# A graph kernel's ending: the flag of odd entries a block earlier, the last rows in two parts

## Chip, cores and metric

The kernel runs on one core of a Trainium2 chip. The metric is the device time of one execution in microseconds (us), the median of several runs. A profile is one execution recorded by the hardware profiler; its times within the execution are counted from the span's start. The engines are TensorE (PE, its weight loads PEld), VectorE (DVE), ScalarE (ACT), GpSimd (POOL) and SyncE (SP).

## The reference

Four graph layers act on x (4096 rows of 64) through one 4096 x 4096 adjacency matrix. Each layer normalizes x, puts the result through ReLU to get h, and adds a term to x. The first three are an attention over the neighbours, a sum over the last 100 neighbours with weights that halve, and a product of h with adj @ h. The last one matters here:

```python
deg = jnp.sum(adj, axis=1, keepdims=True)
nb_agg = adj @ X / jnp.maximum(deg, 1.0)
X_cat = jnp.concatenate([X, nb_agg], axis=1)
out = X_cat @ W.T
return jax.nn.relu(out)
```

Here X is h of layer 3 (layers are numbered from 0) and the result is added to x. The entries of the drawn adjacency are 0 and 1, but the function is defined for any numbers.

## The kernel before

The kernel computes the layers on the assumption that all entries of adj are 0 or 1, and checks this as it goes. Whole-matrix checks on VectorE (`check`, L351) count in a tile `odd` the entries that are neither. At the end `flagged` (L1081 to L1090) sums `odd` over its columns on VectorE (L1084, tile `bad`), over the partitions with a matmul on PE (L1088, tile `pf`), and cuts that down to 0 or 1 on VectorE (L1090, tile `flag`). Each engine then loads `flag` into a register (`values_load`, L1448) and branches (`tc.If`, L1449): if it is 1, the whole model is computed again by a general version, `model(True)`, whose instructions stand between the branch and the end of the program. With the drawn inputs it is 0 and each engine jumps over them. L1495 is where the program ends: every engine drains, and they meet in a barrier.

The 4096 destination rows are worked in 8 blocks of 512 (NIB = 8), numbered 0 to 7 as in the code; so the sixth block is `ib` 5. Layer 3 adds, for each block, 32 products into one PSUM bank (`acc`, L1293), each of 128 x 128 weights with 512 columns of the mask. Blocks 0 to 3 are begun together with a skew of four products; blocks 4 to 7 follow one after the other. When a block's sum is complete, `done3` (L1427) pushes a job, `rows3`, that turns it into 512 rows of output:

- ACT copies and scales `acc` from PSUM to SBUF (`evacuated`, L213)
- PE transposes it in four parts (`turned`, L229)
- ACT copies that to SBUF (L235) and GpSimd adds its two halves (L237): the products are made with numbers split in two parts
- VectorE multiplies by the reciprocal degrees (L1397), GpSimd adds the rows' own term (L1400), VectorE applies ReLU and adds x (L1402)
- GpSimd issues the store (L1403)

For block 7 (`final`) PE does the transposing and the adding of the halves in one, with a constant matrix `fold` (L227), VectorE multiplies straight from PSUM, and SyncE issues the store.

The jobs are Python generators, and the order of instructions on every engine is the order in which these generators emit them. `product` calls `beat` after every fourth product, and `beat` calls `step` (L302). A step advances the jobs in the queue from the front by one `yield` each; a job pushed with a lag of 4 lets no later job run in its first three steps. After the last product, `drain` steps until no job is left. An engine works through its instructions in that order; one that waits holds up all that are queued behind it on the same engine.

`done3` pushes the flag job when block 6 (`NIB - 2`) is complete, after emptying the list of checks. The job yields 12 times between L1084 and L1088. The register is loaded after `model(False)` has returned, behind everything else.

Of the kernel before, what the change touches and what calls it, by code (L numbers as in the profile page):

```python
# [11 lines left out]
F32 = mybir.dt.float32  # L12
# [4 lines left out]
AF = mybir.ActivationFunctionType  # L17
ALU = mybir.AluOpType
# [5 lines left out]
D = 64  # L24
P = 128
NT = N // P
IB = 512
NIB = N // IB
CI = IB // P
# [19 lines left out]
def kernel(  # L49
# [12 lines left out]
    nc = tc.nc  # L62
# [30 lines left out]
    fold = cpool.tile([P, D], F32, name="fold")  # L93
# [8 lines left out]
    part = cpool.tile([P, QUAD], BF16, name="part")  # L102
# [24 lines left out]
    def bc(col, r):  # L127

        return col.unsqueeze(2).to_broadcast([P, r, D])
# [4 lines left out]
    def model(general):  # L134

        sfx = "_g" if general else ""
        stack = ExitStack()

        def pool(name, bufs, on=stack, **kw):
            return on.enter_context(tc.tile_pool(name=name + sfx, bufs=bufs, **kw))  # L140
# [6 lines left out]
        x_sb = main.tile([P, NT, D], F32, name="x_sb" + sfx)  # L147
        fa = main.tile([P, NT, D], F32, name="fa" + sfx)
        rdegs = main.tile([P, NT], F32, name="rdegs" + sfx)
# [35 lines left out]
        epi = pool("epi", 1)  # L185
# [11 lines left out]
        def rows_tile(name, tag, on=epi, bufs=1, dtype=F32):  # L197
            return on.tile([P, CI, D], dtype, tag=name, name=f"{name}{tag}{sfx}", bufs=bufs)

        def small(name, tag, on=epi, n=CI):  # L200
            return on.tile([P, n], F32, tag=name, name=f"{name}{tag}{sfx}")

        def evacuated(ib, acc, layer, scale=None, vector=False, third=False):
            on, bufs = (evac, 1) if third else (epi, 2)
            asb = on.tile([P, IB], F32, tag="asb", name=f"asb{layer}_{ib}{sfx}", bufs=bufs)
            if scale is None:
                nc.scalar.copy(asb, acc)
            elif vector:
                nc.vector.tensor_scalar(asb, acc, scale, None, ALU.mult)
            elif isinstance(scale, float):  # L210
                nc.scalar.activation(asb, acc, AF.Copy, scale=scale)
            else:
                nc.scalar.activation(asb, acc, AF.Identity, scale=scale)  # L213
            return asb

        def turned(asb, b, tag, adding=False):


            shape = (P, CI, D if adding else P)
            if b is None:  # L220
                pt = pm.tile(list(shape), F32, tag="pr", name=f"pt{tag}{sfx}")
            else:
                pt = bank(b, f"pt{tag}", shape)
            for c in range(CI):
                part = asb[:, c * P : (c + 1) * P]
                if adding:
                    nc.tensor.matmul(pt[:, c, :], part, fold, start=True, stop=True)  # L227
                else:
                    nc.tensor.transpose(pt[:, c, :], part, ident)  # L229
            return pt  # L230

        def halves_added(to, asb, pt):

            v = asb.rearrange("p (c i) -> p c i", c=CI)
            nc.scalar.copy(v, pt)  # L235
            yield
            nc.gpsimd.tensor_tensor(to, v[:, :, 0:D], v[:, :, D:P], ALU.add)  # L237
            yield
# [59 lines left out]
        def push(job, lag):  # L298

            jobs.append([job, lag])  # L300
# [20 lines left out]
        def drain():  # L321
            while jobs:
                step()

        def block(ib):
            return slice(ib * CI, (ib + 1) * CI)
# [10 lines left out]
        def check(tiles=1):  # L337


            if not checks:  # L340
                return
            k = checks.popleft()
            ib, t = divmod(k, NT)
            if tiles == 2 and k % 2 == 0:
                checks.popleft()
                at = more[0].tile([P, CG, IB], F32, tag="ckw", name=f"ckw_{k}", bufs=more[1])
                nc.sync.dma_start(out=at, in_=adjt[ib, t // CG])
            else:
                at = ck.tile([P, IB], F32, tag="ck", name=f"ck_{k}", bufs=CHECKED)
                nc.sync.dma_start(out=at, in_=adjt[ib, t // CG][:, t % CG, :])  # L350
            nc.vector.scalar_tensor_tensor(  # L351
                at, at, 0.0, at, ALU.not_equal, ALU.not_equal, accum_out=odd[:, k : k + 1]
            )
# [655 lines left out]
        with tc.manual_schedule():  # L1009
            acc, late = first_rows_and_block()  # L1010
# [19 lines left out]
            for size in sizes:  # L1030
# [10 lines left out]
                for ib, g, att in late:  # L1041
                    at = done % NG
                    if at == 0:
                        acc = pa0.tile([P, IB], F32, tag="pa", name=f"acc0_{ib}{sfx}")
# [6 lines left out]
                late = now  # L1051
# [11 lines left out]
        evac = pool("evac", 1)  # L1063
# [4 lines left out]
        def bank(b, name, shape=(P, IB)):  # L1068
            return banks.tile(list(shape), F32, tag=f"bank{b}", name=name + sfx)
# [11 lines left out]
        def flagged(flag):  # L1081

            bad = small("bad", "")[:, 0:1]
            nc.vector.tensor_reduce(bad, odd, AX.X, ALU.add)  # L1084
            for _ in range(12):
                yield
            pf = pm.tile([P, CI], F32, tag="pr", name="pf")
            nc.tensor.matmul(pf[0:1, 0:1], bad, one, start=True, stop=True)  # L1088
            yield
            nc.vector.tensor_scalar(flag, pf[0:1, 0:1], 1.0, None, ALU.min)  # L1090
# [124 lines left out]
        with tc.manual_schedule():  # L1215
# [42 lines left out]
            late = None  # L1258
            for blocks in GROUPS:
                for k in range(NT // PAIR):  # L1260
                    t = NT - 1 - k * PAIR
# [5 lines left out]
                    late = units, ws  # L1267
# [8 lines left out]
        epi2 = pool("epi2", 1, l2)  # L1276
        stream2 = own_sb = v_sb3 = None
        if general:
            stream2 = pool("stream2", 2, l2)
            own_sb = epi2.tile([P, NT, D], F32, name="own" + sfx)  # L1280
# [28 lines left out]
        def sums(layer, s2, rows32, done, lead, split):  # L1309


            begun = {}
            for n in range(0 if general else split + SKEW * (lead - 1)):
                for ib in range(lead):
                    t = n - SKEW * ib
                    if t == 0:
                        begun[ib] = next_sum(layer, ib)
                    if 0 <= t < split:
                        product(begun[ib], ib, t, s2, layer)
            for ib in range(NIB):  # L1320
                if ib in begun:
                    acc = begun[ib]
                    products23(acc, ib, list(range(split, NT)), s2, rows32, layer)
                else:
                    acc = next_sum(layer, ib)
                    products23(acc, ib, list(range(NT)), s2, rows32, layer)
                done(ib, acc)
                if general:
                    drain()

        sums_level = 1.0 / UP if general else level[:, 1:2]
# [53 lines left out]
        def rows3(ib, acc):  # L1385
            tag = f"3_{ib}"
            rows = block(ib)
            asb = evacuated(ib, acc, 3, sums_level, third=ib % 3 == 2)
            yield
            yield  # L1390
            final = ib == NIB - 1
            pt = turned(asb, 3 + ib % 2, tag, final)
            yield
            y = rows_tile("y", tag, epi2, 2)
            if not final:
                yield from halves_added(y, asb, pt)
            nc.vector.tensor_tensor(y, pt if final else y, bc(rdegs[:, rows], CI), ALU.mult)  # L1397
            yield
            own = (own_sb if general else fa)[:, rows, :]
            nc.gpsimd.tensor_tensor(y, y, own, ALU.add)  # L1400
            yield
            nc.vector.scalar_tensor_tensor(y, y, 0.0, x_sb[:, rows, :], ALU.max, ALU.add)  # L1402
            (nc.sync if ib == NIB - 1 else nc.gpsimd).dma_start(out=out[:, rows, :], in_=y)  # L1403

        def degrees(ib):

# [12 lines left out]
            nc.vector.reciprocal(to, to)  # L1419
            nc.vector.tensor_scalar(to, to, turn_v, None, ALU.mult)  # L1420

        flag = None
        with tc.manual_schedule():
            def done2(ib, acc):
                push(rows2(ib, acc), 6)

            def done3(ib, acc):  # L1427
                nonlocal flag
                push(rows3(ib, acc), 4)
                if ib == NIB - 2 and not general:  # L1430
                    while checks:
                        check(2)
                    flag = cpool.tile([1, 1], I32, name="flag")
                    push(flagged(flag), 1)

            sums(2, s2b, fa, done2, 4, 24)
            if general:
                for ib in range(NIB):
                    degrees(ib)
            often[:] = [True, True, False]  # L1440
            sums(3, s2a, v_sb3, done3, 4, 28)
            drain()
        l2.close()
        stack.close()
        return flag

    flag = model(False)
    any_odd = nc.values_load(flag[0:1, 0:1], min_val=0, max_val=1)  # L1448
    with tc.If(any_odd > 0):  # L1449
        model(True)  # L1450


# [47 lines left out]
```

## Time and profile before

| what | value |
|---|---|
| median of 3 runs | 631.16 us (629.65 to 631.86) |
| the profiled execution | 627.16 us |
| its span | 625.3 us |
| PE busy | 567.6 us (91%) |
| VectorE busy | 482.1 us (77%) |
| ACT busy | 337.4 us (54%) |
| GpSimd busy | 228.2 us (36%) |
| HBM read | 135.63 MB |

The span runs from the first to the last instruction of the profile; the execution takes a little longer. Busy time leaves out waiting and the instructions that only steer: register loads, branches, semaphores, the issuing of DMAs. Two sides of an engine are told apart in the profile: `ACT` is the engine at work, `ACTq` its sequencer, which fetches and issues the instructions. A line such as `pt<-fold,asb 128*128 128x64 f32 x8` names the tile written, the tiles read, the shapes and how many instructions are merged. What stands in brackets behind a line of the timeline is the idle time of the engine before it and what ended that.

### The profile page before, as it was taken

What the parts mean: (1) busy time and instruction counts of PE and PEld (TensorE: products, weight loads), DVE (VectorE), ACT (ScalarE), POOL (GpSimd) and SP (SyncE); (2) the same over time, 40 slices, a digit from 0 to 9 for tenths busy, and PEclk for the clock granted to TensorE, in tenths of its full rate; (3) what the DMA queues carried; (4) which work ended last, traced back from release to release, by engine and by line L of the source; (5) the groups of instructions that cost most, each with busy time, mean ns of one, the idle gap of its engine ahead of it and who ended that gap; (6) DMA issues with size and microseconds to landing.
All of it is one profiled execution on the core that took longest, in us unless ns stands there. A gap on an engine that the chain in (4) does not pass through costs nothing.

```text
span 625.3 us, 9033 instructions
## 1 busy us (share of the span) xinstructions
PE 567.6 (91%) x2997; PEld 230.8 (37%) x3012; DVE 482.1 (77%) x945; ACT 337.4 (54%) x541; POOL 228.2 (36%) x462
## 2 busy tenths in 40 slices
PE   0767999999999999999998999999989999998993
PEld 0653223333333333323343343343434445443551
DVE  5768558998888888888968767868776769988741
ACT  1467567666666676766615667767765024331320
POOL 7423301665656564733336300101000325442352
PEclk9995999999999999999999999999999999999997
DMA  8992914698999898972276332323334575468911
GB/s 138 141 104 18 105 16 85 101 150 140 159 143 159 140 156 139 144 147 84 85 264 207 108 130 101 135 103 123 113 104 132 176 262 180 160 208 303 327 42 32
DMA packets 43640, 87.03 MB, mean 139 GB/s; under 512 B 5216, under 2 KB 21984, under 8 KB 43584
## 3 DMA queue, kind: packets, MB, share of 16 engines
q1 hardware_dynamic: 24672, 68.53, 32.3%
q0 software_dynamic: 18768, 17.70, 30.2%
q8 instruction: 25, 0.41, 0.3%
q10 hardware_dynamic: 144, 0.13, 0.2%
q14 instruction: 31, 0.25, 0.1%
HBM read 135.63 MB, written 1.05 MB: 219 GB/s over the span
## 4 chain that ended last, share of the span: by engine, by line
PE 69%; DVE 11%; DMA 5%; POOL 5%; ACT 4%; issue 4%; SPq 0%; DVEq 0%; POOLq 0%; ACTq 0%
PE acc L1293 16%; PE ps L908 14%; PE acc L935 13%; PE acc L1223 8%; PE cnt L1185 8%; DMA mask<-adjt_dram 3%; PE cnt L1195 3%; DVE att L927 3%; DVE ckw L351 2%; PE pt L229 2%; ACT ps L914 2%; DVE ck L351 1%; PE ps_h L615 1%; DMA x_sb<-x_dram 1%; PE pr L1099 1%
## 5 line engine op out<-in xcount | busy, mean ns | idle before, releaser
L914 ACT ACTIVATE ps<-ps,att_c,att_a 128x1024 f32<-128x1024 f32 x128 | 146.9, 1176 | 83.1 <-PE ps L908 83.0
L927 DVE TENSOR_TENSOR att<-ps,mask 128x1024 f32<-128x1024 f32 x128 | 155.2, 1221 | 39.4 <-ACT ps L914 36.9
L908 PE MATMUL ps<-qt,kt 64*128 64x512 f32 x512 | 134.4, 633 | 4.9 <-DVE att L927 3.9
L351 DVE SCALAR_TENSOR_TENSOR ckw<-ckw 128x1024 f32<-128x1024 f32 x93 | 119.5, 1299 | 7.5 <-DMA ckw<-adjt_dram 7.4
L935 PE MATMUL acc<-att,fb 128*64 128x512 f32 x512 | 122.5, 605 | 0.7 <-DVE att L927 0.7
L1211 ACT ACTIVATE w<-cnt 128x512 int16<-128x512 f32 x176 | 93.1, 597 | 46.0 <-PE cnt L1195 45.7
L1209 DVE TENSOR_SCALAR w<-cnt 128x512 int16<-128x512 f32 x80 | 53.7, 688 | 34.7 <-PE cnt L1195 34.0
L176 POOL DMA_DIRECT2D mask<-adjt_dram x128 | 70.2, 561 | 20.3 <-DMA mask<-adjt_dram 18.6
L908 PEld LDWEIGHTS ps<-qt,kt 64*128 64x128 f32 x512 | 44.3, 188 | 86.6 <-DVE att L927 40.9
L1185 PE MATMUL cnt<-mask,after 128*128 128x512 fp8e4 x256 | 66.5, 379 | 4.4 <-DVE w L1209 3.9
L1223 PE MATMUL acc<-w,s2a 128*128 128x512 bf16 x241 | 64.1, 382 | 1.9 <-issue 1.6
L935 PEld LDWEIGHTS acc<-att,fb 128*64 128x64 f32 x512 | 31.8, 136 | 81.1 <-issue 76.6
L272 POOL TENSOR_TENSOR xc<-x_sb,st 128x256 f32<-128x256 f32 x24 | 19.1, 794 | 108.4 <-DVE st L269 67.5
L1293 PE MATMUL acc<-mask,s2b 128*128 128x512 fp8e4 x256 | 57.7, 379 | 0.0
L1293 PE MATMUL acc<-mask,s2a 128*128 128x512 fp8e4 x256 | 57.6, 380 | 0.0
L351 DVE SCALAR_TENSOR_TENSOR ck<-ck 128x512 f32<-128x512 f32 x70 | 50.6, 724 | 0.0
L258 POOL TENSOR_TENSOR rs_a<-rs_y 128x4 f32<-128x4 f32 x48 | 17.3, 359 | 88.7 <-DVE rs_y L254 81.0
L1185 PEld LDWEIGHTS <-after 128*128 128x128 bf16 x256 | 24.8, 99 | 33.6 <-issue 6.2
L1293 PEld LDWEIGHTS <-s2b 128*128 128x128 f16 x256 | 25.0, 98 | 27.6 <-issue 0.8
L1293 PEld LDWEIGHTS <-s2a 128*128 128x128 f16 x256 | 24.7, 98 | 27.5
L213 ACT ACTIVATE asb<-acc,level 128x512 f32<-128x512 f32 x24 | 16.1, 692 | 32.1 <-PE acc L1293 32.1
L1223 PEld LDWEIGHTS <-s2a 128*128 128x128 f16 x256 | 19.8, 97 | 29.8 <-issue 14.8
(188 smaller groups left out, 529.8 us busy)
## 6 DMA issues: line engine op xcount, KB each, us to landing
ckw<-adjt_dram SPq DMA_DIRECT2D x93, 512.0 KB, 3.8
ck<-adjt_dram SPq DMA_DIRECT2D x70, 256.0 KB, 5.8
mask<-adjt_dram POOLq DMA_DIRECT2D x128, 128.0 KB, 9.0
x_sb<-x_dram SPq DMA_DIRECT2D x4, 256.0 KB, 8.0
out_dram<-y POOLq DMA_DIRECT2D x7, 128.0 KB, 2.2
w_sb<-wts_dram SPq DMA_DIRECT2D x2, 80.0 KB, 7.7
vec<-vecs_dram ACTq DMA_DIRECT2D x1, 130.5 KB, 6.1
out_dram<-y SPq DMA_DIRECT2D x1, 128.0 KB, 1.9
```

The costliest lines, as they stand in the source:

```text
L176: nc.gpsimd.dma_start(out=masks[ib][:, g * CG : (g + 1) * CG, :], in_=adjt[ib, g])
L272: nc.gpsimd.tensor_tensor(xc, xr, bc(st, CI), ALU.add)
L351: nc.vector.scalar_tensor_tensor(at, at, 0.0, at, ALU.not_equal, ALU.not_equal, accum_out=odd[:, k : k + 1])
L908: nc.tensor.matmul(ps[:, c, :], kt[half, g, :], qts[ib][half, :], start=True, stop=True)
L914: nc.scalar.activation(ps, ps, AF.Sigmoid, bias=att_c, scale=att_a)
L927: nc.vector.tensor_tensor(att, ps, mask, ALU.mult)
L935: nc.tensor.matmul(acc[c * D : (c + 1) * D, :], lhs[:, t, :], rhs[:, c, :], start=(at == 0), stop=(at == NG - 1), skip_group_check=True,)
L1185: nc.tensor.matmul(cnt, after, masks[ib][:, t, :], start=True, stop=True, skip_group_check=True)
L1209: nc.vector.tensor_scalar(w, cnt, 0.0, None, ALU.max)
L1211: nc.scalar.activation(w, cnt, AF.Relu)
L1223: nc.tensor.matmul(accs[ib], both(s2a, t), w, start=(t == NT - 1), stop=False, skip_group_check=True,)
L1293: nc.tensor.matmul(acc, both(s2, t), masks[ib][:, t, :], start=(t == 0), stop=(t == NT - 1), skip_group_check=True,)
```

## The change

- The flag job is pushed when block 5 (`NIB - 3`) is complete, and yields 5 times between L1084 and L1088 where it yielded 12 times.
- Block 6 (`late`) has three yields fewer; its own rows are added by VectorE in place of GpSimd, and its store is issued by SyncE in place of GpSimd.
- Block 7 has a function of its own, `last_rows3`. ACT copies the first 256 columns of `acc`, VectorE the other 256. Then each engine loads the flag into its register. For each half PE folds two parts into a PSUM bank of its own, VectorE multiplies by the degree and adds the own term in one instruction for each 64 columns, applies ReLU and adds x in one for the half, and ACT issues the half's store.
- `tc.If` uses the registers that were loaded there.

The general model gets the same new functions; it isn't executed with these inputs.

```diff
@@ flagged
-            for _ in range(12):
+            for _ in range(5):
                 yield
@@ rows3
+            late = ib == NIB - 2
             asb = evacuated(ib, acc, 3, sums_level, third=ib % 3 == 2)
             yield
-            yield
-            final = ib == NIB - 1
-            pt = turned(asb, 3 + ib % 2, tag, final)
+            if not late:
+                yield
+            pt = turned(asb, 3 + ib % 2, tag)
             yield
             y = rows_tile("y", tag, epi2, 2)
-            if not final:
-                yield from halves_added(y, asb, pt)
-            nc.vector.tensor_tensor(y, pt if final else y, bc(rdegs[:, rows], CI), ALU.mult)
-            yield
+            yield from halves_added(y, asb, pt)
+            nc.vector.tensor_tensor(y, y, bc(rdegs[:, rows], CI), ALU.mult)
+            if not late:
+                yield
             own = (own_sb if general else fa)[:, rows, :]
-            nc.gpsimd.tensor_tensor(y, y, own, ALU.add)
-            yield
+            (nc.vector if late else nc.gpsimd).tensor_tensor(y, y, own, ALU.add)
+            if not late:
+                yield
             nc.vector.scalar_tensor_tensor(y, y, 0.0, x_sb[:, rows, :], ALU.max, ALU.add)
-            (nc.sync if ib == NIB - 1 else nc.gpsimd).dma_start(out=out[:, rows, :], in_=y)
+            (nc.sync if late else nc.gpsimd).dma_start(out=out[:, rows, :], in_=y)
+
+        def last_rows3(ib, acc):
...
+            half = slice(0, H * P)
...
+                nc.scalar.activation(asbs[0][:, half], acc[:, half], AF.Identity, scale=sums_level)
+            nc.vector.tensor_scalar(
+                asbs[1][:, half], acc[:, H * P :], sums_level, None, ALU.mult
+            )
+            if not general:
+                any_odd.append(nc.values_load(flag[0:1, 0:1], min_val=0, max_val=1))
+            yield
+            y = rows_tile("y", f"3_{ib}", epi2, 2)
+            for u in range(2):
+                rows = slice(ib * CI + u * H, ib * CI + (u + 1) * H)
+                pt = bank(3 + u, f"pt3_{ib}_{u}", (P, H, D))
+                for c in range(H):
+                    nc.tensor.matmul(
+                        pt[:, c, :], asbs[u][:, c * P : (c + 1) * P], fold, start=True, stop=True
+                    )
+                for c in range(H):
+                    t = ib * CI + u * H + c
+                    nc.vector.scalar_tensor_tensor(
+                        y[:, u * H + c, :], pt[:, c, :], rdegs[:, t : t + 1], own[:, t, :],
+                        ALU.mult, ALU.add,
+                    )
+                part = y[:, u * H : (u + 1) * H, :]
+                nc.vector.scalar_tensor_tensor(part, part, 0.0, x_sb[:, rows, :], ALU.max, ALU.add)
+                nc.scalar.dma_start(out=out[:, rows, :], in_=part)
@@ done3
-                push(rows3(ib, acc), 4)
-                if ib == NIB - 2 and not general:
+                push(last_rows3(ib, acc) if ib == NIB - 1 else rows3(ib, acc), 4)
+                if ib == NIB - 3 and not general:
                     while checks:
                         check(2)
                     flag = cpool.tile([1, 1], I32, name="flag")
@@ the program's end
-    flag = model(False)
-    any_odd = nc.values_load(flag[0:1, 0:1], min_val=0, max_val=1)
-    with tc.If(any_odd > 0):
+    any_odd = model(False)
+    with tc.If(any_odd[0] > 0):
         model(True)
```

More of the change, by code (lines that the diff above doesn't have):

```diff
@@ L1397, in rows3 @@
-            nc.vector.tensor_tensor(y, pt if final else y, bc(rdegs[:, rows], CI), ALU.mult)
-            yield
-            own = (own_sb if general else fa)[:, rows, :]
-            nc.gpsimd.tensor_tensor(y, y, own, ALU.add)
-            yield
-            nc.vector.scalar_tensor_tensor(y, y, 0.0, x_sb[:, rows, :], ALU.max, ALU.add)
-            (nc.sync if ib == NIB - 1 else nc.gpsimd).dma_start(out=out[:, rows, :], in_=y)
+            yield from halves_added(y, asb, pt)
+            nc.vector.tensor_tensor(y, y, bc(rdegs[:, rows], CI), ALU.mult)
@@ new lines, in rows3 @@
+            if not late:
+                yield
+            own = (own_sb if general else fa)[:, rows, :]
+            (nc.vector if late else nc.gpsimd).tensor_tensor(y, y, own, ALU.add)
+            if not late:
+                yield
+            nc.vector.scalar_tensor_tensor(y, y, 0.0, x_sb[:, rows, :], ALU.max, ALU.add)
+            (nc.sync if late else nc.gpsimd).dma_start(out=out[:, rows, :], in_=y)
+        def last_rows3(ib, acc):
+            own = own_sb if general else fa
+            H = CI // 2
+            asbs = [
+                on.tile([P, IB], F32, tag="asb", name=f"asb3_{ib}_{u}{sfx}", bufs=bufs)
+                for u, (on, bufs) in enumerate(((epi, 2), (evac, 1)))
+            ]
+            half = slice(0, H * P)
+            if general:
+                nc.scalar.activation(asbs[0][:, half], acc[:, half], AF.Copy, scale=sums_level)
+            else:
+                nc.scalar.activation(asbs[0][:, half], acc[:, half], AF.Identity, scale=sums_level)
[4 more added lines that the diff above has]
+                any_odd.append(nc.values_load(flag[0:1, 0:1], min_val=0, max_val=1))
+            yield
+            y = rows_tile("y", f"3_{ib}", epi2, 2)
[15 more added lines that the diff above has]
+                nc.scalar.dma_start(out=out[:, rows, :], in_=part)
@@ L1420, in degrees @@
             nc.vector.tensor_scalar(to, to, turn_v, None, ALU.mult)
-        flag = None
+        flag, any_odd = None, []
         with tc.manual_schedule():
@@ L1444, in model @@
         stack.close()
-        return flag
-    flag = model(False)
-    any_odd = nc.values_load(flag[0:1, 0:1], min_val=0, max_val=1)
-    with tc.If(any_odd > 0):
+        return any_odd
+    any_odd = model(False)
+    with tc.If(any_odd[0] > 0):
         model(True)
```

## The prediction

> **What bounds the kernel now.** I read the page first (PE busy 91%, and 0.3 of the last of the 40 slices), then the chain of waits from 612 us on. Blocks are numbered from 0, so the seventh is block 6. The matrix products end at 613.21; what follows is a chain of single instructions:
>
> ```profile
> 613.30 0.70 ACT asb L213
> ...
> 614.04 1.12 PE pt L227 x8
> ...
> 615.18 0.43 DVE y L1397
> ...
> 615.70 0.72 POOL y L1400
> ...
> 616.44 0.42 DVE y L1402
> 616.87 0.06 DVE flag L1090
> ```
>
> The chain ends 8.4 us before the span does (625.34). What fills that time are sequencer instructions, seen in the answers by line for L1448 (loads), L1449 (branch) and L1495 (end); columns: shortest/median/longest ns, then first and last start in us:
>
> ```profile
> L1448 ACTq TENSOR_LOAD <-flag x1: 465/465/465, 617.0 to 617.0; - x1
> ...
> L1448 SPq TENSOR_LOAD <-flag x1: 543/543/543, 617.3 to 617.3; - x1
> ```
>
> ```profile
> L1449 ACTq COMPARE_BRANCH  x1: 50/50/50, 617.5 to 617.5; - x1
> L1449 PEldq COMPARE_BRANCH  x1: 4502/4502/4502, 617.6 to 617.6; - x1
> ...
> L1449 SPq COMPARE_BRANCH  x1: 45/45/45, 618.6 to 618.6; - x1
> L1449 ACTq EVENT_SEMAPHORE  x1: 17/17/17, 620.3 to 620.3; - x1
> ...
> L1449 POOLq INC_SWDGE_SEM  x1: 782/782/782, 621.2 to 621.2; - x1
> ```
>
> ```profile
> L1495 POOLq DRAIN  x3: 46/107/2433, 622.1 to 625.1; - x3
> L1495 SPq DRAIN  x3: 7/7/13, 623.3 to 624.8; - x3
> ```
>
> Every engine loads the flag (0.47 to 0.54 us), branches over the general model, and does nothing for 2.8 us (ACT) to 4.5 us (PE); then GpSimd needs until 624.5 (INC_SWDGE_SEM 0.78, DRAIN 2.43), SyncE until 623.4, and the closing barrier takes 0.85 us. GpSimd ends this tail.
>
> **What the skill says.** "Runtime: NRT & Kernel Launch", Instruction fetch mechanics: a taken branch to a target outside the window waits for a DMA fetch. The trace agrees: after the branches the instruction queues move 9 packets of 8 KB and 2 of 16 KB. "Advanced Engine Details and Errata", Control Flow Timing, gives about 108 ns for a compare-and-branch; the four short ones here take 45 to 72. "TensorE: Matmul & The Clock Gate", What's actually happening: the clock falls after an idle window of about 3.4 us. The trace agrees that shorter gaps are harmless (last fence). "Perfetto Trace Analysis", Optimizing Scalar/DVE Operations: splitting instructions can let work finish sooner, at a fixed cost each. Here ACT's copy from PSUM takes 585 ns for 512 columns and 372 for 256, so 159 are fixed.
>
> **Part 1, the flag made a block earlier: it adds a wait on PE.** A step runs every fourth product. Block 5's row job is pushed with lag 4, the flag job behind it, so the sum L1084 falls in step 4 of block 6, and its PE matmul L1088, five steps later, in step 1 of block 7. L1402 is in the eighth step of a row job: block 4's job began in step 2 of block 5, so its L1402 is emitted in step 1 of block 6, block 5's in step 8. On VectorE the sum then stands behind the former, and VectorE is late, because GpSimd carries the row jobs one after another, 3.33 us each:
>
> ```profile
> 607.06 0.43 DVE L1402 SCALAR_TENSOR_TENSOR y<-y,x_sb 128x256 f32<-128x256 f32 x1 [0.84 <-POOL y L1400]
> ...
> 607.78 0.56 POOL L1403 DMA_DIRECT2D out_dram<-y  x1 [0.76 <-DVE y L1402]
> ...
> 608.28 0.60 PE L229 MATMUL pt<-ident,asb 128*128 128x128 f32 x4
> ...
> 610.40 0.43 DVE L1402 SCALAR_TENSOR_TENSOR y<-y,x_sb 128x256 f32<-128x256 f32 x1 [0.83 <-POOL y L1400]
> 610.74 0.41 DVE L1084 TENSOR_REDUCE bad<-odd 128x1 f32<-128x256 f32 x1
> 611.12 0.56 POOL L1403 DMA_DIRECT2D out_dram<-y  x1 [0.76 <-DVE y L1402]
> 611.70 0.73 POOL L237 TENSOR_TENSOR y<-asb 128x256 f32<-128x256 f32 x1
> ```
>
> The row at 607.06 is block 4's (GpSimd's stores leave in block order; the last, at 614.45, is block 6's). These lines are from the timeline; brackets give idle time before and what ended it. The sum follows such a row by 0.34 us: 607.40 to 607.81. PE reaches step 1 of block 7 eight products before the transposes of block 6 at 608.28 (step 3): 608.28 - 8 x 0.216 = 606.55. So PE stands at L1088 from 606.55 until 607.86, with all of block 7 behind it; the two passes of L1088 cost about 0.1 more (0.19 in all before, pipelined). PE loses 1.4 us: the products end at 613.21 + 1.4 = 614.6. Low 1.1 (if the first products are already queued in the pipe), high 1.6. The flag's own operation comes after 610.40 + 0.34, at 610.74, and no load of it is reached before 612.4: it makes nobody wait. The checks add nothing: the last one is on VectorE ahead of block 2's final operation, before block 5 ends.
>
> **Part 2, block 6's rows in fewer steps.** Its transposes move one step earlier and its own rows are added by VectorE; SyncE stores. GpSimd still adds the halves, in order at 611.70 to 612.43. VectorE follows with three dependent operations of 0.42 + 0.035: 612.47 to 613.81; SyncE issues the store (0.35) until 614.2. This lies under block 7's products. It frees GpSimd at 612.43 instead of 616.41 (its own issue took 0.56), and puts SyncE's load behind that store; nothing else stands in SyncE's queue, whose last loads for the checks are done by 595 (DMA share 0.06 from there, by the windows).
>
> **Part 3, the last rows.** From the end of the products (T):
> - ACT takes half: 0.692 - (0.585 - 0.372) = 0.48 with a hop of 0.09 and 0.05 behind: T + 0.62. VectorE takes the other half (0.42 for 256 columns) at once. The loads on PE (0.49), ACT (0.47) and VectorE (0.54) lie under this and the folds; uncovered they would cost up to 0.5.
> - PE folds the first half in 0.66 (four of its eight passes), the second 0.44 later: T + 1.28 and 1.72.
> - VectorE: per half two operations on 128x64 and one on 128x128. Nearest rows are 0.226 (L1133) and 0.293 (L829), successive independent starts 0.085 before the end: 0.14 + 0.26 + 0.29 = 0.69 a half: done at T + 2.0 and 2.65. Bounds 0.5 and 0.9 a half.
> - ACT issues two stores; the one issue on its queue took 0.396: T + 3.1.
>
> In place of 0.70 + 1.12 + 0.43 + 0.72 + 0.42 with hops and flag (3.7), then a load (0.5). The stores land 1.9 us after issue, before they are asked for.
>
> **Part 4, the tail.** The registers are loaded before, so each engine branches as its work ends: GpSimd at 613.0, SyncE at 615.5, PE at T + 1.7 = 616.3, VectorE at 617.3, ACT at 617.7. GpSimd's tail from branch to end of DRAIN took 617.5 to 624.5, 7.0: done at 620.0. SyncE from branch to DRAIN took 4.8: ready at 620.3. The three other branches fetch near each other, where five did before. I take 4.0 for PE (4.5 before; its 16 KB packet took 1.90 there, 0.88 to 1.5 elsewhere, so down to 3.4), 2.6 for ACT, 3.0 for VectorE (3.3 before): all resume at 620.3. SyncE asks for their semaphores last, 0.35, then 0.85 of barrier: the end is at 621.5, against 625.34: **3.8 us less**. By parts: behind ACT's branch 7.8 becomes 3.8 (4.0 saved), from T to that branch 4.3 becomes 3.1 (1.2 saved), and the PE wait costs 1.4.
>
> The profiled execution took 627.16 for its span of 625.34, 4.0 below the median 631.16. I carry the difference over: 631.16 - 3.8 = **627.4**.
>
> **Rivals.**
> - *PE doesn't wait* (VectorE is earlier in other executions). For: the backlog is one execution's. Against: its spacing is regular. PE, VectorE and ACT are then ready by 619.0, and SyncE (619.1 to 620.3) sets the end: 620.0 to 621.1, gain 4.7: 626.5. Chance 0.12.
> - *The tail isn't shortened*: GpSimd's DRAIN, whose 2.43 us nothing shown explains, waits for the others, or the fetches do. Then ACT's branch at 617.7 + 7.8 = 625.5: 631.4, no change. Against: GpSimd has nothing left to issue. Chance 0.10. It is also how the change could fail to do what it says.
> - *Slower*: the idle 1.3 us in PE lets the clock fall to half, as it does at the end (0.50 from 620 us on). 28 products remain, 0.216 more each: 6.0 - 3.8 = +2.2: 633.4. It decides from 18 slow products on (18 x 0.216 = 3.8). Against it, gaps of 2.2 and 2.0 us (PEclk is the third column from the end):
>
> ```profile
> 333.00:335.30 2.30, 0.08 (x1) 0.08 (x1) 2.23 (x7) 0.57 (x2) 1.48 (x4) 1.00 0.70 262
> ...
> 565.50:567.60 2.10, 0.12 (x2) 0.09 (x2) 1.65 (x5) 0.00 (x0) 0.00 (x0) 1.00 0.89 273
> ```
>
> Chance 0.04.
>
> **Numbers.** The forecast has 0.74. Its own range: wait 1.1 to 1.6, VectorE's halves 0.5 to 0.9, fetches 0.6 shorter or as before (PE then ends it, 0.5 later), uncovered loads 0.5: gain 2.3 to 4.8, 626.4 to 628.9. With the first rival and the scatter of the runs (629.65 to 631.86) about 0.8 lie between 625.4 and 629.9. This kernel tells 0.3% (1.9 us) from no change: faster 0.83, same 0.13, slower 0.04.
>
> **What would show it.** Right: a PE gap before L1088 ended by L1084 near 607.8; two ACT stores ending near 617.7; the long GpSimd DRAIN over by 620; the span near 621.5. Wrong: no gap at L1088, a clock below 1.00 after it, or a GpSimd DRAIN that still ends last.

## The result, and the profile after

The changed kernel takes 627.02 us (median of 13 runs, 624.30 to 628.34), the kernel before 629.19 in the same series (13 runs, 626.80 to 632.59). The ratio is 0.9955 with a 95% interval of 0.9932 to 0.9977: 2.8 us less (1.4 to 4.3; the two medians alone lie 2.2 apart). Forecast were 3.8 us less and 627.4 us. That the absolute number fits better than the gain is luck: the longer series put the kernel before 2 us below the 631.16 that the forecast started from, and this made up for the gain that was missing.

The profiled execution of the changed kernel has a span of 626.3 us, 1.0 *longer* than that of before. The two executions differ ahead of the change: layer 1 took 152.2 us in the changed kernel's and 149.1 in the other (the last section comes back to this). So all that follows is measured within layer 3: from its first product to its last, and from the end of the last product, T, to the end of the span (T is 613.20 before, 618.55 after).

| kernel | layer 3's products | T to end | sum |
|---|---|---|---|
| before | 65.58 | 12.14 | 77.72 |
| changed | 66.85 | 7.78 | 74.63 |
| difference | +1.27 | -4.36 | -3.09 |

The first difference, 1.27, is the wait that the change adds on PE. The timeline of the changed kernel, PE and VectorE around it (brackets: idle time before, and what ended it):

```profile
610.97 0.42 DVE L1406 SCALAR_TENSOR_TENSOR y<-y,x_sb 128x256 f32<-128x256 f32 x1 [0.84 <-POOL y L1403]
611.31 0.41 DVE L1084 TENSOR_REDUCE bad<-odd 128x1 f32<-128x256 f32 x1
...
611.78 0.19 PE L1088 MATMUL pf<-one,bad 128*1 128x1 f32 x2 [0.98 <-DVE bad L1084]
...
614.65 0.14 DVE L1090 TENSOR_SCALAR flag<-pf 1x1 int32<-1x1 f32 x1
```

PE sits idle for 0.98 us, with block 7's products queued behind L1088, until VectorE has got through block 4's rows and the flag's sum.

The chain of waits of the changed kernel behind the last product:

```profile
618.65 0.48 ACT asb L1421
619.13 0.04 issue
619.18 0.67 PE pt L1433 x4
619.85 0.03 issue
619.88 0.49 DVE y L1438 x2
...
620.39 0.29 DVE y L1443
620.69 0.39 DVE y L1438 x2
...
621.10 0.29 DVE y L1443
```

It ends at 621.39, T + 2.84, against T + 3.7 before, and neither GpSimd nor the flag is in it. Behind it come two stores by ACT, and the jump (L1489 is the branch here, L1535 the end of the program; columns: shortest/median/longest ns, then first and last start):

```profile
L1444 ACTq DMA_DIRECT2D out_dram<-y x2: 351/586/822, 620.7 to 621.4; - x2
```

```profile
L1489 SPq EVENT_SEMAPHORE  x8: 17/17/17, 624.1 to 624.6; - x8
...
L1489 POOLq COMPARE_BRANCH  x1: 45/45/45, 615.7 to 615.7; - x1
...
L1489 SPq COMPARE_BRANCH  x1: 45/45/45, 619.4 to 619.4; - x1
L1489 PEldq COMPARE_BRANCH  x1: 3635/3635/3635, 619.7 to 619.7; - x1
L1489 DVEq COMPARE_BRANCH  x1: 72/72/72, 621.1 to 621.1; - x1
L1489 ACTq COMPARE_BRANCH  x1: 54/54/54, 622.3 to 622.3; - x1
...
L1489 ACTq EVENT_SEMAPHORE  x1: 17/17/17, 624.8 to 624.8; - x1
```

```profile
L1535 SPq EVENT_SEMAPHORE  x14: 17/28/28, 624.7 to 626.3; - x14
...
L1535 POOLq DRAIN  x3: 46/107/2352, 619.4 to 626.1; - x3
L1535 SPq DRAIN  x3: 7/7/13, 625.4 to 625.8; - x3
```

The engines no longer branch together: GpSimd does so at 615.7, before the last product, and its DRAIN of 2.35 us is over at 621.8. What comes last is SyncE. It branches at 619.4, does nothing until 624.1, and then works through a row of semaphore waits, one every 0.065 us, until its drain at 625.5. A semaphore is a counter that one engine or a store raises and another waits for; the eight that these stores use are taken in turn. Block 6's store and ACT's first store have the seventh and the eighth, so that ACT's *second* store has the first again, and with it the first place in SyncE's row. The last part of that store was reported at T + 5.52 = 624.07, 17 ns before SyncE goes on. The last place in the row is ACT's, which resumed at T + 6.24, 0.6 us before SyncE got to it.

### The profile page after: what moved, and what is told of

Read it like the earlier page. It is cut to its first block, busy times and chain, and to the rows that moved or that the text cites. A ratio compares the mean times of both kernels' runs of the same rounds, so it can differ in the third digit from the quotient of the medians.

```text
span 626.3 us, 9053 instructions
## 1 busy us (share of the span) xinstructions
PE 573.7 (92%) x3012; PEld 232.0 (37%) x3012; DVE 483.8 (77%) x951; ACT 337.1 (54%) x541; POOL 225.4 (36%) x459
## 4 chain that ended last, share of the span: by engine, by line
PE 67%; DVE 14%; DMA 6%; POOL 4%; issue 4%; ACT 4%; SPq 0%; DVEq 0%; POOLq 0%; ACTq 0%
PE ps L908 15%; PE acc L935 14%; PE acc L1293 10%; PE acc L1223 9%; PE cnt L1185 9%; DVE ckw L351 4%; PE cnt L1195 3%; DVE att L927 3%; DMA ckw<-adjt_dram 3%; DMA mask<-adjt_dram 2%; ACT ps L914 2%; PE pt L229 1%; DMA x_sb<-x_dram 1%; PE ps_h L615 1%; PE pr L1099 1%
## 5 line engine op out<-in xcount | busy, mean ns | idle before, releaser
L1223 PE MATMUL acc<-w,s2a 128*128 128x512 bf16 x256 | 67.8, 387 | 0.1
```

The source lines that it names most:

```text
L1223: nc.tensor.matmul(accs[ib], both(s2a, t), w, start=(t == NT - 1), stop=False, skip_group_check=True,)
```

## The experiments

Each kernel was run in a series of runs beside the kernel before. Ratios are to that kernel; the other columns are from one profiled execution each.

| run | median us | ratio (95%) | layer 3's products | T to end |
|---|---|---|---|---|
| changed | 627.02 | 0.9955 (0.9932 to 0.9977) | 66.85 | 7.78 |
| rows alone | 628.80 | 0.9992 (0.9975 to 1.0009) | 65.21 | 11.11 |
| flag alone | 628.12 | 0.9970 (0.9955 to 0.9985) | 67.47 | 9.58 |
| flag two steps later | 625.35 | 0.9929 (0.9909 to 0.9949) | 65.54 | 8.48 |
| block 6's store by ACT | 625.95 | 0.9947 (0.9928 to 0.9965) | 66.51 | 7.57 |
| one store | 625.77 | 0.9941 (0.9919 to 0.9963) | 67.52 | 7.01 |
| seven small loads | 626.96 | 0.9953 (0.9936 to 0.9971) | 67.11 | 7.16 |
| later flag, ACT, one store | 624.27 | 0.9929 (0.9906 to 0.9951) | 65.81 | 7.90 |
| no branch | 620.89 | 0.9861 (0.9838 to 0.9884) | 65.61 | 6.43 |
| PE jumps last (one run) | 625.99 | – | 67.39 | 9.21 |
| all four edits | 624.45 | 0.9921 (0.9900 to 0.9943) | 67.13 | 7.00 |

### The two halves of the change, each alone

Rows alone: the changed kernel with the flag as before.

```diff
-            for _ in range(5):
+            for _ in range(12):
...
-                if ib == NIB - 3 and not general:
+                if ib == NIB - 2 and not general:
...
-                any_odd.append(nc.values_load(flag[0:1, 0:1], min_val=0, max_val=1))
...
+    any_odd = nc.values_load(flag[0:1, 0:1], min_val=0, max_val=1)
```

> The rows' part alone: block 6's fewer steps and the last rows in two parts, the flag made and loaded as in the kernel before. Theory: the chain behind the last product is shorter by about 0.8 us, and the branch and GpSimd's long end follow it as before: the end 11.2 to 11.5 us behind the last product (12.1 before, 7.8 in the changed kernel), gain 0.6 to 0.9 us. Rival (the shorter chain of rows makes the gain): 2 us or more of the 2.8 measured.

The end came 11.11 us behind T, 1.03 less than before and a little more than expected. The timed runs don't tell this kernel from the one before (0.5 us less; the interval runs from 1.6 less to 0.6 more). All five branches lie within 0.6 us again, and GpSimd's end follows them:

```profile
L1488 POOLq COMPARE_BRANCH  x1: 45/45/45, 616.9 to 616.9; - x1
...
L1488 SPq COMPARE_BRANCH  x1: 45/45/45, 617.5 to 617.5; - x1
...
L1488 POOLq INC_SWDGE_SEM  x1: 771/771/771, 620.5 to 620.5; - x1
```

The rival, 2 us or more from a shorter chain of rows alone, falls.

Flag alone: the kernel before with the flag of the changed one.

```diff
-            for _ in range(12):
+            for _ in range(5):
...
             asb = evacuated(ib, acc, 3, sums_level, third=ib % 3 == 2)
+            if ib == NIB - 1 and not general:
+                any_odd.append(nc.values_load(flag[0:1, 0:1], min_val=0, max_val=1))
...
-                if ib == NIB - 2 and not general:
+                if ib == NIB - 3 and not general:
...
```

> The flag's part alone: the flag made with block 5 and loaded ahead of the last rows, rows as in the kernel before. Theory: GpSimd still adds the last rows' own term, branches about 3.2 us behind the last product, and its 7.0 us to the end of its DRAIN follow: the end 10.8 to 11.2 us behind the last product, 1.1 less than before, while PE waits 1.2 to 1.3 for the flag's sum: no gain, within 0.5 us of before. Rival (the early load makes the gain by itself): 2 us or more faster than before.

The end came at T + 9.58, not 10.8 to 11.2, and the runs gained 1.9 us (0.9 to 2.8), while PE stood idle for 1.59 us at L1088. The end had been expected about 1.4 us too late. GpSimd did end the tail:

```profile
L1450 POOLq COMPARE_BRANCH  x1: 45/45/45, 619.6 to 619.6; - x1
```

```profile
L1496 POOLq DRAIN  x3: 46/107/2433, 623.5 to 626.5; - x3
```

Its long DRAIN lasted until T + 8.74. But its sequencer branched at T + 2.45, as soon as it had issued the last addition and not when that was done, and it resumed in 2.69 us, where it took 3.37 with five engines branching together. In the tail the early load is the larger part, 2.56 against 1.03. Which part gains more on the whole is not shown: layer 3 and tail together are 0.67 shorter with the flag alone, whose execution had a long wait on PE, and 1.40 with the rows alone, while the runs have it the other way round (1.9 and 0.5, with intervals that overlap). Either alone falls short of the two together (3.09 in the traces). The rows' part is worth more on top of the early load than alone (1.80 against 1.03 in the tail): it takes GpSimd and the last store's engine out of the tail's end.

### The wait at L1088

```diff
-            for _ in range(5):
+            for _ in range(7):
```

> The changed kernel with the flag's matmul two steps later on PE (7 yields for 5). Theory: PE's wait at L1088, about 1.26 us in the changed kernel, goes to under 0.1; but SyncE, which ends the changed kernel's tail and hangs on block 6's rows and not on the products, keeps its time, so the span ends no more than 0.4 us earlier than in the changed kernel, and the time from the last product to the end grows from 7.8 to about 8.7 us. Rival (the wait lies on the path that sets the end): the whole 1.26 us is gained, and the end stays 7.8 us behind the last product.

The wait is gone: L1088 starts with no idle time worth a bracket, and layer 3's products are back at 65.54.

```profile
611.50 0.19 PE L1088 MATMUL pf<-one,bad 128*1 128x1 f32 x2
```

But T to end grew from 7.78 to 8.48, so that 0.6 of the 1.3 us is left in the two traces. The ratios say 1.6 us, with intervals that overlap. So neither number that was expected came. Two paths took a part back. One leads over VectorE:

```profile
616.10 0.43 DVE L1399 TENSOR_TENSOR y<-y,rdegs 128x256 f32<-128x256 f32 x1 [1.59 <-POOL y L237]
616.56 0.42 DVE L1403 TENSOR_TENSOR y<-y,fa 128x256 f32<-128x256 f32 x1
617.02 0.42 DVE L1406 SCALAR_TENSOR_TENSOR y<-y,x_sb 128x256 f32<-128x256 f32 x1
617.37 0.48 DVE L1422 TENSOR_SCALAR asb<-acc,level 128x256 f32<-128x256 f32 x1
```

Here T is 616.12, so block 6's rows, held up by GpSimd's queue, end 1.3 us behind the last product, and the copy of block 7's half stands behind them. The second store was issued at T + 3.31 (2.87 in the changed kernel), and its issue took 1.53 us. The other leads over SyncE, as the theory had it: behind block 6's late store it branched at T + 3.05 and went on 3.19 us later, at T + 6.24. The second store's semaphore had been complete for 65 ns by then; where a store held SyncE in the other traces, it went on after 16 or 17 ns. So both paths ended within 65 ns here, and the trace doesn't tell them apart.

### What holds SyncE

Block 6's store issued by ACT behind its load, SyncE issuing nothing:

```diff
-            (nc.sync if late else nc.gpsimd).dma_start(out=out[:, rows, :], in_=y)
+            if late:
+                held.append((rows, y))
+            else:
+                nc.gpsimd.dma_start(out=out[:, rows, :], in_=y)
...
+            for rows, y in held:
+                nc.scalar.dma_start(out=out[:, rows, :], in_=y)
```

> The changed kernel with block 6's store issued by ACT behind its register load, SyncE issuing none. Theory: SyncE branches about 3 us earlier, its wait for the instructions ends before the other engines', and ACT becomes the last: the end comes 7.2 to 7.4 us behind the last product where it was 7.8, a gain of about 0.5 us; PE's wait stays at 1.2 to 1.3. Rival (the tail is bound by the instruction fetches in common, whoever is first): the end stays 7.8 us behind the last product.

SyncE branched 2.6 us before T, and went on only at T + 5.31, 7.9 us later. The jumps of the other engines took 2.5 to 4.6 us in these runs; SyncE waited for the last store's landing again (T + 5.29). The end came at 7.57, between theory and rival, and my theory fell: SyncE's own jump was not what it waited for in the changed kernel. The next two kernels test the new one.

One store for both halves:

```diff
-                nc.scalar.dma_start(out=out[:, rows, :], in_=part)
+            nc.scalar.dma_start(out=out[:, block(ib), :], in_=y)
```

> The changed kernel with one store of all 512 rows by ACT where two stores of 256 were. Theory (new, from the changed kernel's trace: SyncE's row of waits begins with the semaphore of the last store, and that store is held up by PE's instruction fetch): one store waits on the semaphore that SyncE asks for eight places later, and ACT has no second issue of 0.8 us to make; SyncE's row of waits begins before the store has landed, and the end comes 6.8 to 7.2 us behind the last product (7.8 in the changed kernel), a gain of 0.6 to 1.0. Rival (two stores are of use, since half the rows leave 0.7 us sooner): the end 7.8 or later.

Seven small loads:

```diff
+                    spot = cpool.tile([1, 8], F32, name="spot")
+                    for k in range(7):
+                        nc.sync.dma_start(out=spot[0:1, k : k + 1], in_=vecs[0:1, k : k + 1])
```

> The changed kernel with seven loads of 4 bytes by SyncE, behind the pushing of the flag job, that do nothing but move the stores seven semaphores on, so that the last store's is the eighth that SyncE asks for and not the first. Theory (the order of SyncE's waits sets the end): the last store lands and is issued as before, 5.3 to 5.6 us behind the last product, SyncE arrives 0.4 to 0.5 us sooner, and the end comes at 7.2 to 7.4. Rival (SyncE's jump or ACT's sets the end whatever the order): 7.7 or more.

Both came out as expected or better, at 7.01 and 7.16. SyncE's first eight waits after the branch, with one store and with seven loads:

```profile
L1489 SPq EVENT_SEMAPHORE  x8: 17/17/17, 622.3 to 623.6; - x8
```

```profile
L1492 SPq EVENT_SEMAPHORE  x8: 17/17/17, 621.2 to 623.3; - x8
```

In the changed kernel these eight took 0.5 us, all of them behind the landing. Here they are stretched to 1.3 and 2.1 us: SyncE does the first of them while the last store is still under way, and waits for it at the eighth. Now the row's last place counts, ACT's. With one store:

```profile
L1489 ACTq EVENT_SEMAPHORE  x1: 17/17/17, 624.5 to 624.5; - x1
```

```profile
L1535 SPq EVENT_SEMAPHORE  x14: 17/28/232, 623.6 to 625.4; - x14
```

The wait of 232 ns is that for ACT, which resumed at T + 6.03; the longest of these waits was 28 ns in the changed kernel. With the seven loads it is 279 ns (ACT at T + 6.18). In both, SyncE drains 0.09 us after ACT has resumed. In the changed kernel it drained 0.64 after, so the order of asking cost that kernel 0.55 us, up to the point where ACT's jump takes over. The seven loads change nothing else that counts; the second issue took 0.67 and not 0.82. Half the rows leaving sooner, as the rival of the one store had it, gained nothing. The timed runs tell neither kernel from the changed one; so small a part shows in the traces alone.

### Why the second store takes so long to issue

One more matmul on PE that reads the end of the output tile, so that PE branches last but for ACT:

```diff
                 nc.scalar.dma_start(out=out[:, rows, :], in_=part)
+            if not general:
+                px = pm.tile([P, CI], F32, tag="pr", name="px")
+                nc.tensor.matmul(px[0:1, 0:1], y[:, CI - 1, D - 1 : D], one, start=True, stop=True)
```

> The changed kernel with one more matmul on PE of one column, which reads the last rows of the output tile and is not used, so that PE branches behind VectorE's last operation. Theory (PE's instruction fetch of 16 KB holds up one of 16 DMA engines, and with it ACT's second issue): the second store is issued in 0.33 to 0.45 us (0.82 in the changed kernel) and all its parts start together; PE resumes at 6.3 to 7.0 us behind the last product. Rival (the second issue is long because it follows the first): 0.7 us or more as before.

```profile
L1444 ACTq DMA_DIRECT2D out_dram<-y x2: 338/344/351, 617.2 to 617.9; - x2
...
DMA to landing us min/median/max: 1.7/2.9/4.1
```

The second issue took 0.34 us, as the theory had it. That the parts would start together was wrong, and so was PE's time (it resumed at T + 7.36, not 6.3 to 7.0): PE's fetch, one packet of 16 KB, now fell on the second store (packet from T + 4.16 to 5.91), 9 of the store's 144 packets moved only from 5.91 on, and the store landed 4.1 us after its issue, the first one 1.7. In the changed kernel PE's fetch lies at T + 2.17 to 3.30, and the second issue ran from 2.87 to 3.69. In the kernel with the rows alone, where no engine jumps so early, both issues took 0.34 to 0.36 and both landings 1.6 to 1.7.

The other traces agree. In the four with two stores of the halves and PE's fetch across the second issue, that issue ended 0.4 to 0.5 us behind the fetch:

| run | PE's fetch ended, T + | second issue, T + | it took |
|---|---|---|---|
| changed | 3.30 | 2.87 to 3.69 | 0.82 |
| seven small loads | 3.17 | 2.87 to 3.54 | 0.67 |
| block 6's store by ACT | 3.57 | 2.87 to 3.96 | 1.09 |
| flag two steps later | 4.38 | 3.31 to 4.84 | 1.53 |

Where the two halves leave in one store, a fetch lies across that issue too (with one store from 2.15 to 3.22), and it took 0.36 us. So it takes both, a fetch that is under way and a store issued just before; that the second issue is long because it follows the first is not enough. In the store that landed late, the fetch held up those 9 of 144 packets, the share of one of 16 DMA engines. How a fetch holds up an issue is not shown.

### What the branch still costs

Without flag, load and branch; left out are the decision on odd entries and the second computation:

```diff
-            if not general:
-                any_odd.append(nc.values_load(flag[0:1, 0:1], min_val=0, max_val=1))
...
-                    push(flagged(flag), 1)
...
-    any_odd = model(False)
-    with tc.If(any_odd[0] > 0):
-        model(True)
+    model(False)
```

> The changed kernel without the flag, its load and the branch: it leaves out the decision on odd entries and the second computation that hangs on it. Theory: no jump, no instruction fetch beside the stores, the last store issued in 0.35 us and landed 4.5 us behind the last product; with SyncE's waits behind it the end comes at 6.0 to 6.5 us, and PE doesn't wait for the flag's sum: so the branch still costs the changed kernel 1.3 to 1.8 us in the tail. Rival (the early load has hidden the branch whole): 7.5 or more.

The end came at T + 6.43, and the products took 65.61: 1.35 and 1.24 us less than in the changed kernel, 2.6 together, as expected. (The last store was issued in 0.50 us and landed at T + 5.07, not in 0.35 and at 4.5; a fetch of 8 KB lay across this issue without any jump.) The runs show 6 us (620.89 against 627.02), from four runs only. The profiled execution was the slowest of the four (623.32), so the trace doesn't show where the other 3 us lie; that stays open.

### A better version

The three edits are the later flag and the one store, as above, and ACT copying both halves:

```diff
-            nc.vector.tensor_scalar(
-                asbs[1][:, half], acc[:, H * P :], sums_level, None, ALU.mult
-            )
+                nc.scalar.activation(asbs[1][:, half], acc[:, H * P :], AF.Identity, scale=sums_level)
```

> The changed kernel with three edits: the flag's matmul two steps later, both halves of the last sum copied by ACT, one store. Theory: no wait at L1088 (1.0 to 1.6 us of PE back), VectorE no longer copies behind block 6's rows, and the store as in the run with one store: the end 7.0 to 7.6 us behind the last product, 1.6 to 2.4 us less in all than the changed kernel. Rival (block 6's rows on VectorE and GpSimd take the place of the wait): 0.8 us or less.

The end came at 7.90, outside what I had expected, though PE didn't wait; layer 3 and tail together are 0.9 us shorter than in the changed kernel, not 1.6 to 2.4. Here the first theory does hold: block 6's store left at T + 0.64, SyncE's load and branch stood behind it (T + 2.28), and SyncE went on at 5.65, which no store explains: the last one was complete at 5.34, and is asked for eighth. Then came its 1.4 us of waits. So block 6's store was moved to ACT as above, all four edits in one kernel:

> The kernel with the later flag, ACT's copies and one store, and block 6's store moved to ACT behind its load, so that SyncE hangs on no row. Theory (in the run before SyncE's load stood behind block 6's store, and its jump ended last): SyncE branches before the last product, waits only for the last store to land (5.1 to 5.4 us behind the last product) and asks for 14 more semaphores: the end at 6.8 to 7.2 us (7.9 in the run before, 7.8 in the changed kernel), with no wait of PE at L1088: about 2 us less than the changed kernel in layer 3 and the tail together. Rival (ACT's jump or the fetches take SyncE's place): 7.7 or more.

```profile
L1493 SPq EVENT_SEMAPHORE  x8: 17/17/17, 618.0 to 621.8; - x8
...
L1493 SPq COMPARE_BRANCH  x1: 45/45/45, 614.4 to 614.4; - x1
```

With T at 616.59, SyncE branches 2.2 us before it and has done seven of its waits before the store lands. The end came at T + 7.00, and L1088 doesn't wait. Layer 3's products took 67.13 nevertheless: in this execution the clock was at half speed for 3.4 us of them (last section), which can cost up to half of that, 1.7 us by estimate. SyncE's last wait is ACT's again (137 ns), so that ACT's issue and jump are what ends this kernel. The median is 624.45 us, the ratio to before 0.9921: 5.0 us less than before, about 2 less than the changed kernel; the intervals of the two ratios overlap a little. The runs don't tell it apart from the kernel with three edits (0.9929); by its tail it is 0.9 us ahead.

## Why the prediction was right, and where it wasn't

**The wait on PE** was forecast at 1.4 us (1.1 to 1.6) with a gap ended by the flag's sum. It came: 0.98 us idle, 1.27 in the length of layer 3. Each of the six kernels profiled with the sum and the matmul in these steps has it, 0.98 to 1.88 us long, so the phase between PE and VectorE is not the same in every execution, and a forecast from one execution is near by luck in part. In all six the last product ends 6.83 us after the sum: as long as PE waits there, its time hangs on VectorE. Moving L1088 by two steps takes it away.

**Block 6's rows** were forecast under the products, the store's issue ending 0.4 us before T; it ended at T - 0.40.

**The last rows** were forecast to let ACT branch at T + 3.1; it did at T + 3.72. VectorE's halves took 0.80 each and not 0.69 (within the bounds): the operation on 128x64 takes 0.28 with its operands in PSUM, and the second starts 0.20 after the first, not 0.14. The rest is the second issue, 0.82 where 0.40 was taken. VectorE didn't copy its half at once: it began 34 ns after ACT had ended; but when ACT copied both, nothing came sooner.

**The tail** was forecast to lose GpSimd as its end and to have jumps of 4.0 (PE), 3.0 (VectorE) and 2.6 us (ACT); these took 3.69, 2.93 and 2.52, and GpSimd's DRAIN was over 3.2 us behind T. The step that failed is "The stores land 1.9 us after issue, before they are asked for", and with it "SyncE asks for their semaphores last, 0.35". The second store landed 2.64 us after the start of its issue, SyncE asked for it *first*, and had its whole row of 1.42 us still to go. It was forecast ready at T + 5.7, with 0.35 to come, and arrived at T + 6.95. That is 0.9 us of the tail (7.78 where 6.9 was forecast). Of this the order of asking is 0.55, by the experiments; the rest goes with ACT, which resumed 0.54 later than forecast. With the wait 0.1 shorter than forecast it makes 3.1 us of the 3.8. The mechanism of the gain was right, and its size came out about a fifth smaller in the trace and a quarter in the runs.

**The rivals.** PE did wait; the tail was shortened; the clock didn't fall after L1088 in any of these traces. But the gaps of 2.2 and 2.0 us, from which the forecast took that shorter gaps are harmless, don't show that, and the last of the rivals was nearer than its chance of 0.04 says (last section).

## What to carry to other kernels

If a kernel ends with a branch on a value that it computed, make the value early and load it into the registers ahead of the last work: the jump of each engine, 2.5 to 4.6 us here, then overlaps with what the others still do, and an engine with a long end of its own (GpSimd, 6 to 7 us from its branch) is given its last work first. Then look at who is asked for at the very end and in which order: a store that is waited for first, ahead of a row of waits that were long fulfilled, costs up to the length of the row (0.55 of 1.42 us here, because another engine was late as well). A small instruction moved forward into another engine's queue can hold up all that is queued there: count on which engine its input is made, and how late that engine runs.

## What was unexpected of the hardware

Idle gaps of about 2 us in PE can cost clock. The prediction took gaps of 2.2 and 2.0 us at full clock for a sign that they are harmless. In the changed kernel's execution they weren't: after gaps of 2.47 and 1.78 us, both in layer 1, the clock stood at half for 3.41 us each time. At the same two places the execution of before had gaps of 2.22 and 1.41 and kept its clock.

What decides is not the length of the gap alone. In all twelve traces the granted clock changes only at points of a grid, 3.41 us apart; in the changed kernel at 335.99, 339.40, 472.52 and 475.94, which are 1, 39 and 1 steps from each other. Cut along this grid, these are the stages of the changed kernel around its two gaps (the first pair after the length is PE's busy time, the third column from the end the granted clock):

```profile
332.58:335.99 3.41, 1.36 (x7) 0.32 (x6) 3.27 (x11) 1.76 (x4) 1.78 (x3) 1.00 0.88 302
335.99:339.40 3.41, 2.98 (x10) 0.80 (x10) 2.80 (x5) 1.37 (x3) 2.67 (x10) 0.50 0.65 187
469.11:472.52 3.41, 1.63 (x10) 0.51 (x9) 3.33 (x7) 0.88 (x2) 0.00 (x0) 1.00 0.31 90
472.52:475.94 3.42, 3.42 (x13) 0.94 (x11) 1.59 (x4) 1.65 (x5) 0.00 (x0) 0.50 0.66 214
```

and those of the kernel before around its gap of 2.22:

```profile
330.85:334.27 3.42, 2.15 (x16) 0.61 (x9) 3.28 (x9) 2.17 (x4) 1.86 (x2) 1.00 0.88 281
334.27:337.68 3.41, 2.41 (x13) 0.90 (x13) 3.24 (x7) 1.49 (x3) 2.75 (x9) 1.00 0.67 209
```

In the changed kernel PE was idle for 2.05 and 1.78 us of one step, and the next step ran at half. In the kernel before the gap lay across a point of the grid, 1.27 and 0.95 us on its two sides, and nothing came of it. From 70 us to the last product, every step at full clock with more than 2.0 us of idle PE was followed by half clock (7 in the twelve traces), and none with less than 1.78; of those between, 4 were and 4 were not. So a gap costs clock if enough of it falls into one step, and where the grid lies is chance. The longest waits at L1088, 1.59 and 1.88 us, put 1.47 and 1.58 into one step.

In four of the twelve profiles layer 1 has no half-clock step and took 149.1 to 149.6 us; in eight it has one or two and took 150.8 to 152.7, the longer gaps themselves included. So one to three microseconds come and go between executions, as much as the change brings. "TensorE: Matmul & The Clock Gate" of the Trainium skill, What's actually happening, gives about 3.4 us for the idle window; these traces don't let one read that as a safe length for a gap. Their grid has that step, but a step with 1.8 to 2.0 us of idle time could be enough.

PE's sequencer runs far ahead: in the changed kernel its register load took place at 614.83, as soon as the flag was made, 3.7 us before its last product ended. So the load cost PE nothing at all.
